# The second image's 3x3 convolution in tiles of 4 by 4 outputs instead of 4 by 2

## The chip, the cores and the metric

The kernel runs on one core of a Trainium2 chip. The time of a run is the device time of that core in microseconds; the time of a kernel is the median of its runs. A profile is one further execution, recorded by the hardware profiler.

Names of engines in what follows: PE is TensorE's matmuls and PEld its weight loads, DVE is VectorE, ACT is ScalarE, POOL is GpSimd, and SP is SyncE, which here only issues transfers.

## What is computed

Four images of 256 channels and 64 by 64 pixels, in fp32, go through four layers. Each layer normalises its input by groups of eight channels (`_gn`) and adds its result to it. Cut to what matters:

```python
# layer 0: a 3x3 convolution, group norm, relu, then attention over all 4096 pixels
xs = conv_general_dilated(x, smooth_w, (1, 1), padding='SAME') + smooth_b
xs = relu(group_norm(xs, gn1_w, gn1_b))
theta_x, phi_x, g_x = conv1x1(xs, ...)            # 128 channels each
attn = softmax(einsum('bnc,bcm->bnm', theta_x, phi_x))
y = einsum('bnm,bmc->bnc', attn, g_x)
x = x + group_norm(conv1x1(y, w_w, w_b)) * 0.1 + xs
# layer 1: linear attention; layer 2: generated depthwise and pointwise
# convolution; layer 3: a mixture of four 1x1 convolutions
```

The 3x3 convolution of layer 0 is what the change is about.

## The kernel before, in words

**Rounds.** The 256 channels are two halves of 128 partitions. Image 0's convolution runs first and alone (`convolve_first`), the prologue. Then come four rounds. Round b holds the attention of image b (`attend`): 8 blocks of 512 queries, each in 16 steps. A step makes two logits products `pf`, their exponentials `pr` on ACT (into `k4` buffers of 1024 elements), two products `py` with `g`, and adds `pr` to a running total `tot` on DVE. After a block, a product with ones sums `tot` over the partitions (`pss`), DVE takes the reciprocal and scales `py` into `yt`, and two products `ps_wy` follow; their statistics are taken on DVE and the result goes to `wy_d` in HBM.

**What runs beside the attention.** The order of every engine's work is written out by hand (`manual_schedule`): the engines take their instructions in program order. A `Chain` is a generator that yields prices; each unit of price times the chain's rate is one attention step. `later(n, f)` emits `f` after n further steps. In round 0 the chain is `scale_weights` and the convolution of image 1 at rate 1.5; in rounds 1 and 2 it is the rest of the layers of image b-1 (`tail`) and the convolution of image b+1 at rate 0.86; in round 3 the tail of image 2. The tail of image 3 runs alone at the end. Between the rounds `project` makes theta, phi and g from the convolved image in `big`.

**The convolution** (`convolve`) is of the Winograd kind: 4 output rows by 2 output columns at a time, that is 6 by 4 positions (`TY, MY, TX, MX = 6, 4, 4, 2`). For each of six row positions a, `down` combines input rows into `ra` (with `rt` between) on DVE. For each of four column positions k, `across` makes the moving operand `v` (two halves of 512) with one DVE operation:

```python
first, second, op = ((0, 2, ALU.subtract), (1, 2, ALU.add), (2, 1, ALU.subtract), (1, 3, ALU.subtract))[k]
tt(v.rearrange("p (h y x) -> p h y x", h=NH, x=IX), col(first), col(second), op)
```

`products` multiplies v by the transformed filters u: 2 output halves by 2 input halves, 4 matmuls of 512 columns into two banks, line 403:

```python
for oh in range(NH):
    for h in range(NH):
        nc.tensor.matmul(ps[oh], u(oh, h), v[:, bass.ts(h, 512)], start=(h == 0), stop=(h == NH - 1))
```

`joined` adds the four products into even and odd columns, and `joining` combines the six row positions into the four output rows in `big` (`image`). The emission of a product comes one step after its v, and its join one step later (`w.later(1, ...)`). DVE operations go through the helpers `tt` (line 118) and `stt` (line 121), so these two lines stand for many operations; the tile names tell them apart. `stats` (line 393) takes the statistics for the group norm, and `normed_relu` (line 492, ACT) finishes the image, each part of which is added to `xs_d` in HBM by a POOL transfer.

**Filters.** The transformed filters are made in the prologue from the 3x3 filters: `filter_down` makes the six rows `u1` (in `tpg`), and `filter_across` makes of each row the four column positions (lines 277 and after: one ACT and three DVE operations of 512 elements) and stores them in `filters` in HBM with eight transfers of 128 KB from SP. The prologue convolves image 0 in two forms: rows 3 and 4 with `products`, rows 0, 1, 2 and 5 with `row_products` (line 435; three horizontal taps in place, u1 as weights, copied from PSUM by ACT at line 440). Its v for row 3 is read from `rc`, a part of `big`. In rounds 0 to 2 `load_filters` brings the two u tiles of a product from `filters`, one product ahead.

Of the kernel before, what the change touches and what calls it, by code (L numbers as in the profile page):

```python
# [13 lines left out]
P = 128  # L14
# [20 lines left out]
TY, MY, TX, MX = 6, 4, 4, 2  # L35
IY, IX = HW // MY, HW // MX

# [53 lines left out]
def conv_preact_fast(ctx: ExitStack, tc: tile.TileContext, guard, x, wc, wtpg, ww, wqkv, wout, w1cat, wd2,  # L91
# [11 lines left out]
    def k4(name):  # L103
        return wk.tile([P, CH], F32, tag="k4", name=name, bufs=10)
# [3 lines left out]
    def k2(name):  # L108
        return wk.tile([P, 512], F32, tag="k2", name=name, bufs=6)
# [18 lines left out]
    big = cp.tile([P, NH, N], F32, name="big")  # L128
    tpg = cp.tile([P, 3, N], F32, name="tpg")
    ra = cp.tile([P, NH, IY, HW + 2], F32, name="ra")  # L130
    rt = cp.tile([P, NH, IY, HW], F32, name="rt")
# [24 lines left out]
    bigf = big.rearrange("p h n -> p (h n)")  # L156
# [79 lines left out]
    filters = tc.dram_tile([TY, NH, P, TX, NH, P], F32, name="filters")  # L236
# [30 lines left out]
    def filter_across(a, stay=False):  # L267

        ends = u1[:, a].rearrange("p h (j o) -> p h j o", j=3)
        s, mid = (t.rearrange("p (h o) -> p h o", h=NH)  # L270
                  for t in (wk.tile([P, 512], F32, tag="inv", name="ends2"), k2("middle") if a == 4 else junk()))
        if stay:
            both = [k2("both_u").rearrange("p (h o) -> p h o", h=NH) for _ in range(2)]
        else:
            t = k4("both_u").rearrange("p (b h o) -> p b h o", b=2, h=NH)
            both = [t[:, b] for b in range(2)]
        nc.scalar.mul(mid, ends[:, :, 1], 0.5)
        tt(s, ends[:, :, 0], ends[:, :, 2], ALU.add)
        stt(both[0], s, 0.5, mid, ALU.mult, ALU.add)
        stt(both[1], s, 0.5, mid, ALU.mult, ALU.subtract)  # L280

        def of(k):
            return both[k - 1] if k in (1, 2) else ends[:, :, 0 if k == 0 else 2]

        for oh in range(NH):
            for k in range(TX):
                nc.sync.dma_start(out=filters[a, oh, :, k], in_=of(k)[:, :, bass.ts(oh, P)])
        return lambda k, oh, h: of(k)[:, h, bass.ts(oh, P)]

# [60 lines left out]
    def rows_of(k, h=None):  # L350

        sel = slice(k, k + MY * (IY - 1) + 1, MY)
        return xp[:, :, sel, :] if h is None else xp[:, h, sel, :]
# [4 lines left out]
    def down(a, to, prior=None):  # L358

        A, T = inside(to), rt  # L360
        mul, add, sub = ALU.mult, ALU.add, ALU.subtract
        if a in (0, 5):
            lo = 0 if a == 0 else 1
            return [(stt, o, i, f, j, mul, add) for h in range(NH) for o, i, f, j in (
                (A[:, h], rows_of(lo + 2, h), -5.0, rows_of(lo + 4, h)), (A[:, h], rows_of(lo, h), 4.0, A[:, h]))]
# [6 lines left out]
        return [(stt, A[:, h], T[:, h], -2.0 if a == 2 else -4.0, inside(prior)[:, h], mul, add) for h in range(NH)]  # L372

    def across(k, rows):

        def col(j):
            return rows[:, :, :, j:j + MX * (IX - 1) + 1:MX]

        v = k4("v")
        first, second, op = ((0, 2, ALU.subtract), (1, 2, ALU.add), (2, 1, ALU.subtract), (1, 3, ALU.subtract))[k]  # L380
        tt(v.rearrange("p (h y x) -> p h y x", h=NH, x=IX), col(first), col(second), op)
        return v

    ACROSS = (1, 2, 0, 3)

    def joiner(st):
# [8 lines left out]
        def take(a, oh):  # L395
            dst[oh] = image[:, oh, :, a, :] if a in (0, 1, 3) else k4("t").rearrange("p (y x) -> p y x", x=HW)

        def products(a, k, v, u):

            ps = [bank("ps_conv") for _ in range(NH)]  # L400
            for oh in range(NH):
                for h in range(NH):
                    nc.tensor.matmul(ps[oh], u(oh, h), v[:, bass.ts(h, 512)], start=(h == 0), stop=(h == NH - 1))  # L403
                if k == 1:
                    one[oh] = k2("one").rearrange("p (y x) -> p y x", x=IX)
                    nc.scalar.copy(one[oh], ps[oh].rearrange("p (y x) -> p y x", x=IX))
            return ps

        def joined(a, k, ps):

            for oh in range(NH):
                p = ps[oh].rearrange("p (y x) -> p y x", x=IX)
# [3 lines left out]
                if k == 2:  # L416
# [26 lines left out]
        def joining(a, oh, t):  # L443

            y0, y1, y2, y3 = (image[:, oh, :, j, :] for j in range(MY))
            if a == 2:
                return [(tt, y2, y1, t, ALU.add), (tt, y1, y1, t, ALU.subtract), (tt, y0, y0, y2, ALU.add)]
            if a == 4:
                both = k4("both").rearrange("p (y x) -> p y x", x=HW)
                return [(tt, both, y3, t, ALU.add), (tt, y3, y3, t, ALU.subtract), (tt, y0, y0, both, ALU.add),  # L450
                        (stt, y2, both, 4.0, y2, ALU.mult, ALU.add), (stt, y1, y3, 2.0, y1, ALU.mult, ALU.add),
                        (stt, y3, y3, 6.0, y1, ALU.mult, ALU.add)]
            return [(tt, y3, y3, t, ALU.add)] if a == 5 else []

        def rows_joined(a, oh, t):
            for op, *args in joining(a, oh, t):
                op(*args)

        return products, joined, row_products, rows_joined, joining, stats

    def input_stats():
# [6 lines left out]
        return (yield from group_finish(st, avg8, 1e-5))  # L468

# [14 lines left out]
    def normed_relu(w, b, st):  # L484
# [3 lines left out]
        sc, sh = affine(gm, rstd, vec_s[:, V_G1W, :], vec_s[:, V_G1B, :], bias, 1.0)  # L488
        for c in range(N // CH):
# [6 lines left out]
    def convolve(w, b):  # L496

        _, gm, rstd = yield from input_stats()
        yield from normalise(gm, rstd)
        st = stats_tile()  # L500
        products, joined, _, rows_joined, joining, stats = joiner(st)
        PRODUCTS = [(a, k) for a in range(TY) for k in ACROSS]

# [32 lines left out]
        def load_filters(i):  # L536
            res = []
            for oh in range(NH):
                u = wk.tile([P, NH, P], F32, tag="u", name="u", bufs=4)
                nc.sync.dma_start(out=u, in_=filters[PRODUCTS[i][0], oh, :, PRODUCTS[i][1]])  # L540
                res.append(u)
            return lambda oh, h: res[oh][:, h, :]
# [3 lines left out]
        for i, (a, k) in enumerate(PRODUCTS):  # L546
            if k == 1:
                for op, *args in down(a, ra, ra):
                    op(*args)
                    yield 0.35  # L550
            v, u = across(k, ra), us
# [7 lines left out]

    def convolve_first(w):  # L560
# [5 lines left out]
        def across_all(a, rows):  # L566
            return [(a, k, across(k, rows), lambda oh, h, k=k: u[a](k, oh, h)) for k in ACROSS]

# [4 lines left out]
        products, joined, row_products, rows_joined, _, stats = joiner(st)  # L573
        go(down(0, ra))
        filter_down((1, 2))
        go(down(1, rb))
        filter_down((5,))
        filter_down((3, 4))
        u = {a: filter_across(a, stay=True) for a in (4, 3)}
# [6 lines left out]
        go(down(2, ra, rb))  # L586
        row_products(1, rb)
        go(down(3, rc))
        three = [(a, k, products(a, k, v, u)) for a, k, v, u in across_all(3, rc)]
        go(down(4, rb, rc))  # L590
        four = across_all(4, rb)
        go(down(5, rb))
        for i, (a, k, v, f) in enumerate(four):
            if i + 1 < TX:
                joined(*three[i + 1])
            filter_across((0, 1, 2, 5)[i])
# [3 lines left out]
        for i in range(1, TX):  # L600
# [460 lines left out]
    def mixed(w, b, big, k4, st, sh, held):  # L1061
# [39 lines left out]
        for h in range(NH):  # L1101
            wm.append(mix[:, h, :] if held is None else wk.tile([P, NH * P], F32, tag="u", name="wmh", bufs=4))
# [69 lines left out]
    with tc.manual_schedule(engines={E.PE, E.Activation, E.DVE, E.Pool, E.SP}):  # L1172
        run(Chain(convolve_first).steps())
        run(project())
        for b in range(B - 1):
            attention = attend(b)
            parts = [tail(b - 1, big, qT)] if b > 0 else [scale_weights]
            if b == 0:
                load_x(1)
            run(Chain(both(*parts, lambda w: convolve(w, b + 1)), 1.5 if b == 0 else 0.86).steps(), attention)  # L1180
# [605 lines left out]
```

## Time and profile before

| what | value |
|---|---|
| median of 3 runs | 3144.82 us (3144.27 to 3144.91) |
| the profiled execution | 3145.76 us, of which its span 3144.0 us |
| granted TensorE clock | 0.987 of full, mean over the span |
| prologue, up to the first `ps_tp` of image 0 | 146.1 us |
| round 0, first `pf` to the first `ps_tp` of image 1 | 190.9 to 738.5 us |
| `tot` on DVE, 1024 elements | x448, mean 1219 ns |
| `v` on DVE, 1024 elements | x72, mean 1219 ns |
| reciprocal on DVE, 512 elements | x32, mean 3352 ns |
| joins from PSUM on DVE, 512 elements | 682 to 684 ns |
| normalise on DVE, 1024 elements | x16, mean 807 ns |

How to read the page: a group row names line, engine, operation, output <- input by the program's names, shape and count, then busy time and the mean of one, then the engine's idle time before it and what ended that. Durations include a latency that overlaps the next instruction, so the distance from one start to the next is shorter than the mean of one. The chain of waits is followed back from the last instruction, each time to what released it. fp32 matmuls count two instructions each.

### The profile page before, as it was taken

The page shows a single profiled execution, that of the slowest core. Times are in us where ns is not written, and L with a number is a line of the kernel's source. Part 1 is how long each engine was busy: PE and PEld are TensorE (multiplying, and loading weights), DVE is VectorE, ACT ScalarE, POOL GpSimd, SP SyncE. Part 2 cuts the span into 40 slices and gives each one's busy share as a digit, 9 for nine tenths or more (in the row PEclk, how much of TensorE's full clock was granted, in tenths as well). Part 3 has the DMA queues.
Part 4 walks back from the last instruction along what each step waited for, and adds up shares of the span by engine and source line. Part 5 has one row for each costly group of instructions (what it writes and reads, how often), then busy time and mean ns, then how long its engine had stood idle before and what let it go on. Part 6 is the DMA issues. An engine that isn't in the chain of part 4 may idle for free.

```text
span 3144.0 us, 24213 instructions
## 1 busy us (share of the span) xinstructions
PE 3033.0 (96%) x8526; PEld 1472.9 (47%) x8526; DVE 2079.6 (66%) x2611; ACT 1129.2 (36%) x2097; POOL 131.6 (4%) x175
## 2 busy tenths in 40 slices
PE   6899999999999999999999999999999999996888
PEld 3454444445564444444565444444545544443533
DVE  8736766443547995877536896778363768855485
ACT  2233224332555332323364432222445443333510
POOL 0000000000010000000011000000100100000100
PEclk9999999999999999999999999999999999998999
DMA  5610013001100023113300102310410010120011
GB/s 184 182 34 26 32 35 66 7 14 47 67 11 21 20 74 116 39 39 67 114 8 3 41 20 77 110 44 31 113 62 1 11 34 14 47 74 34 14 60 65
DMA packets 73985, 161.68 MB, mean 51 GB/s; under 512 B 7936, under 2 KB 39424, under 8 KB 70912
## 3 DMA queue, kind: packets, MB, share of 16 engines
q1 hardware_dynamic: 69248, 143.27, 13.3%
q0 software_dynamic: 4608, 16.78, 2.9%
q8 instruction: 70, 1.15, 0.2%
q14 instruction: 59, 0.48, 0.0%
HBM read 103.40 MB, written 73.40 MB: 56 GB/s over the span
## 4 chain that ended last, share of the span: by engine, by line
PE 80%; DVE 12%; issue 5%; ACT 2%; DMA 0%; POOL 0%; SPq 0%; POOLq 0%; ACTq 0%
PE pf L655 23%; PE py L694 23%; PE ps_conv L403 8%; PE ps_qkv L784 5%; DVE dw L121 4%; PE ps_tp L631 4%; PE ps_ex L1117 3%; PE ps_pw L979 3%; DVE tot L118 2%; PE ps_g L636 2%; PE ps_wy L678 2%; PE ps_o L852 1%; PE ps_ctx L806 1%; PE ps_dw L1014 1%; PE ps_ss L770 1%
## 5 line engine op out<-in xcount | busy, mean ns | idle before, releaser
L656 ACT ACTIVATE pr<-pf 128x512 f32<-128x512 f32 x1024 | 604.2, 596 | 1227.3 <-PE pf L655 1214.2
L655 PE MATMUL pf<-tpg 128*128 128x512 f32 x2048 | 967.2, 595 | 1.4 <-ACT pr L656 1.4
L694 PE MATMUL py<-pr,tpg 128*128 128x512 f32 x2048 | 962.1, 592 | 3.0 <-ACT pr L656 2.9
L118 DVE TENSOR_TENSOR tot<-tot,pr 128x1024 f32<-128x1024 f32 x448 | 546.3, 1219 | 249.7 <-ACT pr L656 248.1
L694 PEld LDWEIGHTS py<-pr,tpg 128*128 128x128 f32 x2048 | 388.8, 190 | 494.3 <-issue 479.8
L655 PEld LDWEIGHTS pf<-tpg 128*128 128x128 f32 x2048 | 381.5, 190 | 443.0 <-issue 419.1
L121 DVE SCALAR_TENSOR_TENSOR dw<-xp,dk,dw 128x1008 f32<-128x1008 f32 x216 | 272.9, 1267 | 6.8 <-ACT dw L971 3.7
L403 PE MATMUL ps_conv<-v,u 128*128 128x512 f32 x576 | 259.0, 596 | 3.6 <-DVE v L118 3.6
L403 PEld LDWEIGHTS ps_conv<-v,u 128*128 128x128 f32 x576 | 109.7, 191 | 143.5 <-issue 136.6
L784 PE MATMUL ps_qkv<-wqkv_s,xg 128*128 128x384 f32 x384 | 129.9, 487 | 0.0
L631 PE MATMUL ps_tp<-big,wtpg_s 128*128 128x512 f32 x256 | 118.0, 605 | 3.0 <-ACT big L492 3.0
L118 DVE TENSOR_TENSOR tpg<-ps_g,bg_s 128x512 f32<-128x512 f32 x32 | 22.1, 691 | 145.6 <-PE ps_g L636 145.6
L210 POOL TENSOR_TENSOR rstd<-rstd,half 128x2 f32<-128x2 f32 x24 | 16.8, 700 | 2419.3 <-DVE rstd L315 2225.7
L979 PE MATMUL ps_pw<-dw,pk 128*128 128x512 f32 x224 | 104.6, 601 | 8.1 <-DVE dw L121 8.1
L669 DVE RECIPROCAL inv<-pss 128x512 f32<-128x512 f32 x32 | 107.3, 3352 | 7.2 <-PE pss L667 7.2
L784 PEld LDWEIGHTS ps_qkv<-wqkv_s,xg 128*128 128x128 f32 x384 | 72.2, 190 | 53.6 <-issue 9.6
L794 DVE TENSOR_REDUCE qs<-qk 128x16 f32<-128x512 f32 x24 | 16.5, 686 | 119.0 <-ACT qk L788 119.0
L118 DVE TENSOR_TENSOR v<-ra 128x1024 f32<-128x1024 f32 x72 | 86.7, 1219 | 0.4
L632 ACT ACTIVATE tpg<-ps_tp,btp_s 128x512 f32<-128x512 f32 x64 | 43.9, 687 | 119.6 <-PE ps_tp L631 119.6
L631 PEld LDWEIGHTS ps_tp<-big,wtpg_s 128*128 128x128 f32 x256 | 47.9, 195 | 55.0 <-issue 50.6
L854 ACT ACTIVATE junk<-ps_o 128x256 f32<-128x256 f32 x128 | 49.2, 384 | 67.5 <-PE ps_o L852 59.4
L979 PEld LDWEIGHTS ps_pw<-dw,pk 128*128 128x128 f32 x224 | 43.0, 192 | 62.6 <-issue 51.9
(281 smaller groups left out, 2904.6 us busy)
## 6 DMA issues: line engine op xcount, KB each, us to landing
u<-filters SPq DMA_DIRECT2D x144, 128.0 KB, 2.3
xp<-in_x_dram SPq DMA_DIRECT2D x16, 1024.0 KB, 6.3
xs_d<-big POOLq DMA_DIRECT2D x32, 512.0 KB, 11.7
wy_d<-wt SPq DMA_DIRECT2D x32, 512.0 KB, 3.0
out_dram<-res SPq DMA_DIRECT2D x64, 256.0 KB, 2.0
wy<-wy_d SPq DMA_DIRECT2D x28, 512.0 KB, 5.2
xs<-xs_d SPq DMA_DIRECT2D x24, 512.0 KB, 5.3
wp<-in_wp_dram SPq DMA_DIRECT2D x16, 512.0 KB, 4.6
```

What stands on the lines that cost most here:

```text
L118: nc.vector.tensor_tensor(o, a, b, op)
L121: nc.vector.scalar_tensor_tensor(o, a, s, b, op0, op1)
L403: nc.tensor.matmul(ps[oh], u(oh, h), v[:, bass.ts(h, 512)], start=(h == 0), stop=(h == NH - 1))
L631: nc.tensor.matmul(ps, wtpg_s[:, h, k, :], big[:, h, cols], start=(h == 0), stop=(h == NH - 1))
L636: nc.tensor.matmul(ps[:, j, :], big[:, h, bass.ts(4 * c + j, P)], wtpg_s[:, h, 2, :], start=(h == 0), stop=(h == NH - 1))
L655: nc.tensor.matmul(pf, phi[:, bass.ts(2 * m + s, P)], theta[:, bass.ts(q, 512)], start=True, stop=True)
L656: nc.scalar.activation(pr[:, bass.ts(s, 512)], pf, AF.Exp)
L669: nc.vector.reciprocal(inv, pss)
L694: nc.tensor.matmul(py, g[:, bass.ts(2 * m + s, P)], probs[i][:, bass.ts(s, 512)], start=(m == 0 and s == 0), stop=(m == NM - 1 and s == 1))
L784: nc.tensor.matmul(ps[:, 0:3 * HID], xg[:, h, bass.ts(j, P)], wqkv_s[:, h, :], start=(h == 0), stop=(h == NH - 1))
L979: nc.tensor.matmul(ps, pk[:, h * NH * P + oh * P:h * NH * P + (oh + 1) * P], dw[h][:, bass.ts(s, 512)], start=(h == 0), stop=(h == NH - 1))
L1117: nc.tensor.matmul(ps, wm[h][:, bass.ts(oh, P)], big[:, h, cols], start=(h == 0), stop=(h == NH - 1))
```

## The change

Only image 1's convolution (round 0) changes its form; images 2 and 3 keep 4 by 2 tiles. It takes 6 by 6 positions, in three pairs of column positions, (1,2), (3,4) and (0,5). The normalised input is written to `big` in a new place and order: every fourth pixel side by side (`planar`), so that a column position is 16 consecutive elements. The outputs go to where the input was (`xp`), and the last Relu puts them back in order into `big`. One set of filters serves both forms: `filter_across` for rows 0, 1, 2 and 5 and all stores of `filters` leave the prologue, which stores the six rows `u1` in `rows_d` instead (`keep`). `filters_across`, in round 0 ahead of the convolution, loads them back into `big`, makes four column positions of each on DVE, and stores these; the two outer ones are read from `rows_d`. The 4 by 2 form takes positions 0, 1, 2 and 3, of which 1 and 2 now carry a factor 0.5 at the join. Tiles u are of 512 elements and three, not of 256 and four; `k4` has 9 buffers for 10, `k2` has 5 for 6. `big` grows to (64+2) rows of 68. The chain of round 0 gets the rate 1.22.

```diff
-TY, MY, TX, MX = 6, 4, 4, 2
+TY, MY, TX, MX = 6, 4, 6, 4
 IY, IX = HW // MY, HW // MX
+TX1, MX1 = 4, 2
+RW = MX * (IX + 1)
...
-        return wk.tile([P, CH], F32, tag="k4", name=name, bufs=10)
+        return wk.tile([P, CH], F32, tag="k4", name=name, bufs=9)
...
-    big = cp.tile([P, NH, N], F32, name="big")
+    big_all = cp.tile([P, NH, (HW + 2) * RW], F32, name="big")
+    big = big_all[:, :, 0:N]
...
+    def filters_across(w):
+        n = NH * 3 * NH * P
+        def load(a):
+            t = big[:, a % 2, 0:n].rearrange("p (h j o) -> p h j o", h=NH, j=3)
+            nc.sync.dma_start(out=t, in_=rows_d[a])
+            return t
+        loaded = [load(0), load(1)]
+        yield 2
+        for a in range(TY):
+            t = loaded[a]
+            f = big[:, a % 2, n:n + (TX - 2) * NH * NH * P].rearrange("p (k h o) -> p k h o", k=TX - 2, h=NH)
+            first, mid, last = (t[:, :, j, :] for j in range(3))
+            for op, *args in ((tt, f[:, 0], first, last, ALU.add), (tt, f[:, 1], f[:, 0], mid, ALU.subtract),
+                              (tt, f[:, 0], f[:, 0], mid, ALU.add), (stt, f[:, 2], last, 4.0, first, ALU.mult, ALU.add),
+                              (stt, f[:, 3], mid, -2.0, f[:, 2], ALU.mult, ALU.add),
+                              (stt, f[:, 2], mid, 2.0, f[:, 2], ALU.mult, ALU.add)):
+                op(*args)
+                yield 0.3
+            if a + 2 < TY:
+                loaded.append(load(a + 2))
+            nc.sync.dma_start(out=filters[a], in_=f)
...
+        ops = {0: lambda: each(2, -5.0, col(4), col(5)) + each(0, 4.0, vt[:, 0], vt[:, 1]),
+               1: lambda: each(1, -4.0, col(3), col(4)) + [(tt, one, one, two, add), (stt, two, two, 2.0, one, mul, sub)],
+               3: lambda: [(tt, vt, cols(3), cols(1), sub), (stt, one, one, 2.0, two, mul, add),
+                           (stt, two, two, 2.0, one, mul, sub)]}
...
+        def products(pair, v, u):
+            banks = []
+            for i in range(2):
+                ps = bank("ps_conv")
+                for oh in range(NH):
+                    for h in range(NH):
+                        nc.tensor.matmul(ps[:, bass.ts(oh, IY * IX)], u[i][:, h, bass.ts(oh, P)],
+                                         v[:, i, bass.ts(h, IY * IX)], start=(h == 0), stop=(h == NH - 1))
+                banks.append(ps)
+            if pair != (0, 5):
+                parts[pair] = k4("sums").rearrange("p (k n) -> p k n", k=2)
+                nc.scalar.mul(parts[pair][:, 0], banks[0], -1 / 6 if pair == (1, 2) else 1 / 24)
+            return banks
...
+            if pair == (0, 5):
+                put((0, 0.25, ps[0], None), (3, 1.0, ps[1], None))
+            elif not end:
+                s = parts[pair]
+                f = -1 / 6 if pair == (1, 2) else 1 / 24
+                stt(s[:, 1], ps[1], -f, s[:, 0], ALU.mult, ALU.add)
+                stt(s[:, 0], ps[1], f, s[:, 0], ALU.mult, ALU.add)
+            else:
+                near, far = parts[1, 2], parts[3, 4]
+                put(*((j, f, far[:, j % 2], near[:, j % 2]) for j, f in enumerate((1.0, 2.0, 4.0, 8.0))))
...
+    def normalise_planar(gm, rstd):
...
+                src = xin[:, h, rows, :].rearrange("p y (i r) -> p y r i", r=MX)
+                to = planar[:, h, rows.start + 1:rows.stop + 1, :].rearrange("p y (r i) -> p y r i", r=MX)[:, :, :, 0:IX]
+                if h == 0:
+                    nc.vector.tensor_scalar(to, src, gm[:, 0:1], rstd[:, 0:1], ALU.subtract, ALU.mult)
+                else:
+                    nc.scalar.activation(to, src, AF.Identity, bias=nb[:, h:h + 1], scale=rstd[:, h:h + 1])
+            yield 1
...
+    def convolve_second(w):
...
+            elif a == 4:
+                for oh in range(NH):
+                    rest.extend(joining(a, oh, dst[oh]))
+                for j in range(4):
+                    w.later(1 + j, lambda: some(3))
+                for j in range(3):
+                    w.later(5 + j, lambda j=j: stats(j))
...
+            if pair == PAIRS[0]:
+                for op, *args in down(a, planar, ra, rt, ra):
+                    op(*args)
+                    yield 0.75
...
+            for op, *args in ops:
+                op(*args)
+                yield 0.4
+            w.later(1, lambda a=a, pair=pair, v=v, u=u: multiply(a, pair, v, u))
+            yield 1
...
-            parts = [tail(b - 1, big, qT)] if b > 0 else [scale_weights]
+            parts = [tail(b - 1, big, qT), lambda w: convolve(w, b + 1)] if b > 0 else [
+                scale_weights, filters_across, convolve_second]
...
-            run(Chain(both(*parts, lambda w: convolve(w, b + 1)), 1.5 if b == 0 else 0.86).steps(), attention)
+            run(Chain(both(*parts), 1.22 if b == 0 else 0.86).steps(), attention)
```

In the built program all engines' instructions keep the order in which this code emits them.

## The prediction

> **What bounds the kernel now.** I read the page first, then busy time by stretch of round 0 (the attention of image 0, with the convolution of image 1 beside it; 190.9 us is its first logits product, 738.5 us the end of its last), then the timelines of the waits found there.
>
> ```profile
> PE 3033.0 (96%) x8526; PEld 1472.9 (47%) x8526; DVE 2079.6 (66%) x2611; ACT 1129.2 (36%) x2097; POOL 131.6 (4%) x175
> PE 80%; DVE 12%; issue 5%; ACT 2%; DMA 0%; POOL 0%; SPq 0%; POOLq 0%; ACTq 0%
> L403 PE MATMUL ps_conv<-v,u 128*128 128x512 f32 x576 | 259.0, 596 | 3.6 <-DVE v L118 3.6
> ```
>
> ```profile
> 190.90:310.00 119.10, 119.10 (x284) 53.32 (x283) 78.96 (x95) 43.58 (x72) 0.71 (x1) 1.00 0.05 16
> 380.00:390.00 10.00, 8.10 (x20) 3.40 (x19) 10.00 (x10) 2.39 (x4) 0.00 (x0) 1.00 0.00 0
> 460.00:470.00 10.00, 8.35 (x21) 3.45 (x20) 9.93 (x9) 2.39 (x4) 0.00 (x0) 1.00 0.01 2
> 500.00:738.50 238.50, 238.50 (x560) 105.73 (x559) 105.56 (x105) 94.12 (x156) 7.65 (x9) 1.00 0.12 27
> ```
>
> The columns are the stretch, its length, then busy time of PE, PEld, DVE, ACT, POOL. PE is busy for all of round 0's 547.6 us but 3.55 us. Both holes lie where DVE is busy throughout, and both end with a v:
>
> ```profile
> 374.82 2.48 DVE L118 TENSOR_TENSOR big<-big,t 128x1024 f32<-128x1024 f32 x2
> 377.21 1.22 DVE L118 TENSOR_TENSOR ra<-xp 128x1024 f32<-128x1024 f32 x1
> 378.34 1.22 DVE L118 TENSOR_TENSOR rt<-xp 128x1024 f32<-128x1024 f32 x1
> 379.48 1.22 DVE L118 TENSOR_TENSOR tot<-tot,pr 128x1024 f32<-128x1024 f32 x1
> ...
> 388.56 1.22 DVE L118 TENSOR_TENSOR v<-ra 128x1024 f32<-128x1024 f32 x1
> ```
>
> ```profile
> 389.83 5.40 PE L403 MATMUL ps_conv<-v,u 128*128 128x512 f32 x8 [1.90 <-DVE v L118]
> ```
>
> So a matmul taken out of round 0 comes off the time, unless DVE, which serves the attention's totals and the convolution in one queue, falls behind.
>
> **PE work removed.** The old image 1 needs 24 products of 4 matmuls, 192 instructions of 512 columns (each fp32 matmul is two). The chain of waits has 8 of them in 3.43 us, 0.4292 us each: 82.4 us. The new one needs 6 by 6 positions by 4 matmuls by 2: 288 instructions of 256 columns. The nearest rows with another width scale with columns (the chain has 16 of ps_qkv, 384 columns, in 5.16 us; 16 of ps_g, 128 columns, in 1.78 us), so 0.2146 us each: 61.8 us. Gain **20.6 us**. [...] ps_g's 16 instructions, each with its own load of 128 columns, advance by 111 ns, and this does not hold the load's 192 ns as well. 256-column ones exist too, eight in 1.83 us to the next matmul, the first after a wait:
>
> ```profile
> 925.54 1.99 PE L852 MATMUL ps_o<-w,xp 128*128 128x256 f32 x8 [0.52 <-DVE w L121]
> 927.37 1.88 PE L655 MATMUL pf<-tpg 128*128 128x512 f32 x4
> ```
>
> I take 20.6.
>
> **Old waits of round 0**: both holes belong to the old order of DVE's work, and go: -3.6 us. What is late next follows.
>
> **New DVE work of round 0.** Down stays 24 operations, on 1088 elements for 1024. Across is 66 operations for 24. The joins, counted in the built order, are 24 on sums, 42 on the outputs in xp and 14 on rt, most of 512 elements. Filters_across adds 36 of 512 elements. From the starts above, an independent operation on 1024 advances DVE by 1.14 us (1.25 if it needs the one before), one on 512 by 0.61, so one on 1088 by 1.21. Together DVE rises from some 310 to 361 us, against some 527 us of PE: it has room on the average, and filters_across (three operations a step of 3.43 us, 1.8 us beside 1.14 of totals) and normalise_planar (one operation a step) are hidden. The latter reads every fourth fp32; no row has that. [...] The old v reads every second fp32 and costs the 1219 ns of a plain one[...]. The old row of this step is 0.81 us; even at 2.4 us it fits the 2.2 us that a step leaves, nearly, so I take nothing. The last Relus stand five steps (17 us) ahead of image 1's projection, in the built ScalarE order, so their strides are covered as well.
>
> Room on the average is not enough at one place. In the built order the twelve joins of row 4 and the statistics come right after the seventh query block's reciprocal. From there to the first half of row 5's first v, DVE has: reciprocal 3.39, yt 0.61, twelve joins of 1024 (six dependent) 14.3, two downs 2.4, three totals 3.4, two statistics of wt 1.2, three v operations 1.9: 27.2 us, starting 0.2 us after the reciprocal's product. PE has six steps of 3.43 and ps_wy's 1.72: 22.3 us. PE waits **5.1 us**. Then DVE has the rest of that v 0.7, three totals 3.4, twelve statistics 7.3, the next pair's difference and two operations 2.4, a pair of sums 1.5: 15.3 us, against PE's 3.43 + 6.87 + 1.72 = 12.0: **3.2 us** more. The same addition on the old order gives 2.0 and 1.7 us where the trace has 1.9 and 1.65, so I trust it to about 2 us. Elsewhere DVE's arrears stay under two steps. Sum +8.3 us; queued behind on DVE are the totals and the next reciprocal, and nobody else waits long.
>
> **The filters' way through HBM.** Keep stores the six rows (4.7 MB) in the prologue, in place of 48 stores of 128 KB on SP. Filters_across loads and stores some 11 MB through SP in about 45 us, 245 GB/s. Each DVE operation there waits in order for its load, with the totals behind it. In 100 to 120 us the trace moves 395 GB/s, and between 200 and 240 us now nothing, so I take 0; at the 187 GB/s of 80 to 100 us, the row with the most small transfers, each of six rows would be about 2.3 us late, less what slack holds: up to 5 us on PE. A pair needs two u tiles and there are three, so the second load of the next pair waits on SP for the current pair's first product, and a wy_d store may stand behind it. The next pair comes some three steps (10 us) later, and u's 128 KB land in 2.3 us, so this costs nothing.
>
> **Prologue.** Filter_across for rows 0, 1, 2, 5 leaves: 12 DVE operations of 0.61 and four of ScalarE, and their DMAs. PE runs without a hole from 47.8 to 137.3 us there, so this gains nothing. But the built program has one wait more. The first v of row 3 now waits for ScalarE's eighth copy of row products, which the old one did not (big's planes lie 4488 elements apart instead of 4096; the code gives no need for it).
>
> ```profile
> 63.49 0.59 ACT L440 COPY big<-ps_row 128x512 f32<-128x512 f32 x1 [4.56 <-PE ps_row L435]
> 68.64 0.59 ACT L440 COPY big<-ps_row 128x512 f32<-128x512 f32 x1 [4.56 <-PE ps_row L435]
> 70.36 0.59 ACT L406 COPY one<-ps_conv 128x512 f32<-128x512 f32 x1 [1.13 <-PE ps_conv L403]
> ```
>
> The old v is done by 60.3 us, the new one starts at 69.3 and ends at 70.5; PE was to go on at 68.4. **+2.1 us.** The other v behind it (1.14 each against PE's 3.43) catch up.
>
> **Rounds 1 and 2.** The factor 0.5 turns 24 joins each into scalar forms (683 ns to at most the 748 of the nearest PSUM row), two small memsets enter POOL, and k4 falls from 10 buffers to 9, so some exponentials may wait for a total two or three steps back. PE's idle there is about 7 us a round. I take +0.3 us, bounds 0 and 3.
>
> **Sum**: -20.6 - 3.6 + 8.3 + 2.1 + 0.3 = -13.5 us. The profiled execution has a span of 3144.0 us and 3145.76 us in all; 3144.0 - 13.5 = 3130.5, and 1.8 around it gives 3132.3. The median of the runs is 0.9 us below the profiled one: **3131 us**.
>
> **The rivals.**
> - VectorE keeps up (0.13): its operations overlap better than I add, the 8.3 us vanish: 3131 - 8.3 = 3123 us. For it: DVE is free 34% of the time. Against: the same addition finds the old waits.
> - VectorE or the filters' DMA are later than I add (0.16): up to 5 us by the DMA bound, or 10% dearer short-run operations (42 us of DVE in the critical stretch, so 4 us): about 3136 us.
> - Weight loads show at 256 columns[...] (0.06): [...] Against it are ps_g and ps_o.
> - Slower (0.04): the new operations run over rows of 16 elements, and no row has runs shorter than 32 outputs. The convolution's own DVE operations are some 133 us of 254 in a stretch of 355. At 1.7 times their price the stretch's 92 us of DVE room is used up and DVE becomes the bound; from 1.9 times on (254 + 0.9 x 133 = 374, 19 us over the stretch) the change is slower by more than 0.2%, and at 2.0 times (387, 32 us over) the time is 3163 us. Against: runs of 64 in rows of 66 cost 1219 ns, like flat ones.
> - The case of the sum (0.61): 3126 to 3135 us.
>
> 6.3 us (0.2%) is about what a measurement of this kernel can tell from no change. Below 3138.5 us lie the sum's case, the first rival and most of the second: faster 0.87; same 0.09; slower 0.04. The range, 3123 to 3139 us, reaches from the first rival to the end of the second.
>
> **What would show it.** Right: ps_conv of 256 columns near 0.215 us apart; round 0 about 531 us long; two PE waits on v near the seventh block, together 6 to 10 us, with DVE full; about 2 us of PE idle before the first ps_conv; rounds 1 to 3 as before. Wrong: PE waiting on yt or v early in round 0 (DMA), weight loads between conv matmuls, or v operations on 512 well above 0.69 us.

## The result and the profile after

The changed kernel takes **3126.92 us** (median of four runs, 3125.03 to 3129.2) against 3144.86 us for the kernel before (four runs of the same session, 3144.27 to 3146.62): 0.9942 of the time, 95% interval 0.9925 to 0.996. The forecast was 3131 us. The profiled execution took 3125.03 us, its span 3123.2 us.

The same two lines of the page as in the prediction, and the new form's row:

```profile
PE 3008.6 (96%) x8622; PEld 1492.7 (48%) x8622; DVE 2122.4 (68%) x2689; ACT 1138.1 (36%) x2101; POOL 130.9 (4%) x178
PE 76%; DVE 16%; issue 6%; ACT 2%; DMA 0%; POOL 0%; SPq 0%; POOLq 0%; ACTq 0%; DVEq 0%
L563 PE MATMUL ps_conv<-v,u 128*128 128x256 f32 x288 | 68.0, 391 | 5.3 <-DVE v L124 5.0
```

PE has 96 instructions more and 24 us less of busy time, and DVE has 43 us more. The 288 new instructions waited once for a v that was late, for 5.0 us.

To see where the time went, I cut the span at four places that all kernels here have: the first logits product `pf`, the first `ps_tp` of image 1 (end of round 0), the last `ps_wy` of image 3, and the end.

| stretch | before | after | difference |
|---|---|---|---|
| prologue, up to the first `pf` | 190.76 | 192.88 | +2.1 |
| round 0 | 547.62 | 529.71 | -17.9 |
| rounds 1 to 3, up to the last `ps_wy` | 2106.45 | 2106.96 | +0.5 |
| last stretch (image 3's last layers, alone) | 299.2 | 293.6 | -5.5 |
| span | 3144.0 | 3123.2 | -20.8 |

The last row but one is a surprise: the change does not touch that code. Up to there the change is worth 15.3 us; the forecast had 13.5.

**Round 0.** First the whole of it, before and after, by engine (columns as in the prediction: stretch, length, busy time of PE, PEld, DVE, ACT, POOL, then granted clock, DMA share, GB/s):

```profile
190.76:738.38 547.62, 544.07 (x1272) 241.00 (x1271) 323.98 (x344) 185.35 (x310) 8.36 (x10) 1.00 0.10 26
```

```profile
192.88:722.59 529.71, 524.45 (x1369) 261.14 (x1368) 373.31 (x434) 197.88 (x318) 7.14 (x9) 0.99 0.20 59
```

DVE's work grew by 49 us (forecast: 51) and is still far below PE's. PE has few holes. Its timeline in the changed kernel, where they are:

```profile
615.07 1.88 PE L933 MATMUL py<-pr,tpg 128*128 128x512 f32 x4
621.98 6.26 PE L563 MATMUL ps_conv<-v,u 128*128 128x256 f32 x16 [5.03 <-DVE v L124]
628.08 1.88 PE L894 MATMUL pf<-tpg 128*128 128x512 f32 x4
...
634.94 1.89 PE L563 MATMUL ps_conv<-v,u 128*128 128x256 f32 x8
637.06 1.97 PE L563 MATMUL ps_conv<-v,u 128*128 128x256 f32 x8 [0.23 <-PE ps_conv L563]
```

DVE's timeline just ahead of the wait's end:

```profile
618.85 2.48 DVE L127 SCALAR_TENSOR_TENSOR xp<-xp 128x1024 f32<-128x1024 f32 x2
621.24 0.69 DVE L124 TENSOR_TENSOR v<-v 128x512 f32<-128x512 f32 x1
```

The last of row 4's twelve joins (`xp<-xp`) stand in DVE's queue right ahead of the v that PE needs, as the prediction said, and the wait is 5.03 us where it had 5.1. The second wait that it had, 3.2 us at row 5's second pair, is only 0.23 us at 637.06. But there is something else: the sixteen products after the wait take 6.10 us from start to next start. Elsewhere in this round sixteen take 3.45 (a line of the chain of waits, then the stretches around the pause). The granted clock, the third column from the end, tells why:

```profile
335.12 3.45 PE ps_conv L563 x16
```

```profile
616.90:620.30 3.40, 0.05 (x1) 0.00 (x0) 3.37 (x4) 0.00 (x0) 0.00 (x0) 1.00 0.00 0
620.30:627.15 6.85, 5.17 (x12) 4.19 (x13) 6.82 (x9) 0.60 (x1) 0.00 (x0) 0.50 0.03 9
```

3.4 us into the pause the clock falls to half, and it stays there for 6.8 us, 5.2 of them with work in hand: 2.65 us lost. The kernel before shows the same on a small scale. After its pause of 1.90 us the eight products at 389.83, shown in the prediction, took 5.24 us to the next start, not 3.43. First the stretch with the pause, then the one at half clock:

```profile
387.30:390.71 3.41, 1.51 (x4) 0.49 (x3) 3.41 (x4) 0.00 (x0) 0.00 (x0) 1.00 0.00 0
390.71:394.12 3.41, 3.41 (x5) 1.33 (x4) 3.41 (x4) 0.59 (x1) 0.00 (x0) 0.50 0.04 13
```

So round 0 adds up: products 82.4 - 62.1 = -20.3; old waits -3.55, and -1.8 for the clock behind the first; new wait +5.03, clock behind it +2.65, and +0.23. Together -17.7, measured -17.9.

**Prologue.** The predicted wait is there. ScalarE's eighth copy, the v behind it, and PE's product that waits for that v:

```profile
69.37 0.58 ACT L535 COPY big<-ps_row 128x512 f32<-128x512 f32 x1 [4.57 <-PE ps_row L530]
```

```profile
69.99 4.64 DVE L124 TENSOR_TENSOR v<-big 128x1024 f32<-128x1024 f32 x4 [10.67 <-ACT big L535]
```

```profile
71.27 7.13 PE L491 MATMUL ps_conv<-v,both_u 128*128 128x512 f32 x16 [1.94 <-DVE v L124]
```

### The profile page after: what moved, and what is told of

Same layout as the page of the kernel before. It is cut to its first block, busy times and chain, and to the rows that moved or that the text cites. A ratio compares the mean times of both kernels' runs of the same rounds, so it can differ in the third digit from the quotient of the medians.

```text
span 3123.2 us, 24290 instructions
## 1 busy us (share of the span) xinstructions
PE 3008.6 (96%) x8622; PEld 1492.7 (48%) x8622; DVE 2122.4 (68%) x2689; ACT 1138.1 (36%) x2101; POOL 130.9 (4%) x178
## 4 chain that ended last, share of the span: by engine, by line
PE 76%; DVE 16%; issue 6%; ACT 2%; DMA 0%; POOL 0%; SPq 0%; POOLq 0%; ACTq 0%; DVEq 0%
PE pf L894 22%; PE py L933 22%; PE ps_qkv L1023 5%; PE ps_conv L491 4%; DVE dw L127 4%; PE ps_tp L870 4%; PE ps_ex L1356 3%; DVE tot L124 3%; PE ps_pw L1218 3%; PE ps_conv L563 2%; PE ps_g L875 2%; PE ps_o L1091 1%; PE ps_wy L917 1%; DVE big L127 1%; PE ps_ctx L1045 1%
## 5 line engine op out<-in xcount | busy, mean ns | idle before, releaser
L491 PE MATMUL ps_conv<-v,u 128*128 128x512 f32 x384 | 170.8, 593 | 0.0
L491 PEld LDWEIGHTS ps_conv<-v,u 128*128 128x128 f32 x384 | 72.9, 190 | 92.0 <-issue 91.1
L563 PE MATMUL ps_conv<-v,u 128*128 128x256 f32 x288 | 68.0, 391 | 5.3 <-DVE v L124 5.0
```

The costliest lines, as they stand in the source:

```text
L563: nc.tensor.matmul(ps[:, bass.ts(oh, IY * IX)], u[i][:, h, bass.ts(oh, P)], v[:, i, bass.ts(h, IY * IX)], start=(h == 0), stop=(h == NH - 1))
```

## The experiments

My theory after this reading: the stage sums hold; what I had left out is the clock, which charged a second time for two pauses (2.65 us behind the one of 5.03 us, 1.8 us behind the one of 1.90 us); and the last stretch's 5.5 us are the clock too, not the change. The rivals are written with each run. All kernels below were profiled, and their stretches are set together here, since totals alone cannot tell effects of 2 us:

| kernel | median of runs | first `pf` | round 0 | rounds 1 to 3 | last stretch |
|---|---|---|---|---|---|
| before, first profile | 3144.86 (4) | 190.76 | 547.62 | 2106.45 | 299.2 |
| before_again | 3144.96 (1) | 191.20 | 545.94 | 2106.45 | 299.6 |
| changed, first profile | 3126.92 (4) | 192.88 | 529.71 | 2106.96 | 293.6 |
| after_again | 3128.74 (5) | 195.12 | 529.71 | 2107.06 | 298.9 |
| no_copy_wait | 3129.88 (5) | 191.28 | 529.72 | 2106.95 | 299.8 |
| fill_new_hole | 3132.74 (5) | 192.24 | 531.39 | 2106.98 | 300.4 |
| spread_joins | 3124.14 (5) | 191.99 | 521.41 | 2106.96 | 299.9 |
| before_filled | 3144.33 (13) | 191.42 | 545.94 | 2106.48 | 296.5 |
| tail_spin | 3128.85 (5) | 193.09 | 529.70 | 2107.03 | 297.5 |
| filters_alone | 3144.72 (13) | 193.07 | 546.04 | 2107.14 | 298.5 |
| split_products | 3133.51 (6) | 192.11 | 531.69 | 2106.98 | 299.6 |
| best | 3119.76 (5) | 191.48 | 521.41 | 2106.92 | 298.2 |
| best_spin | 3119.59 (5) | 190.88 | 521.41 | 2106.92 | 298.6 |

**The changed kernel with PE kept busy in the new hole.** In `products`, ahead of a bank's own matmuls; `extra` is 5 for row 5's first pair and 0 elsewhere.

```diff
+                for _ in range(extra if i == 0 else 0):
+                    nc.tensor.matmul(ps, ones, phi[:, 0:512], start=True, stop=True)
```

> The changed kernel with five more matmuls of 512 columns (4.29 us by the 0.429 us per two instructions of the chain) put on PE ahead of the first product of row 5, the one that waits 5.03 us for v; their result is overwritten. In the profile the 16 products after that wait take 6.1 us where 16 elsewhere take 3.45. Theory: they are slow because the granted clock falls to 0.5 after a pause, so with PE kept busy they take 3.45 us and round 0 ends 2.65 us sooner although work was added: 526.9 us for 529.6, 3124.3 us. Rival: the second half of the pair waits for DVE and the clock has no part: the row takes 6.1 us still, round 0 stays 529.6 us or grows, 3127 us or more.

Measured: round 0 took 531.39 us, 1.7 more, and the runs 3132.74 us (ratio to before 0.9963, 0.995 to 0.9977). PE's timeline:

```profile
616.15 4.46 PE L562 MATMUL ps_conv<-tpg,ones 128*128 128x512 f32 x10
621.34 3.72 PE L565 MATMUL ps_conv<-v,u 128*128 128x256 f32 x16 [0.73 <-DVE v L124]
624.90 1.88 PE L896 MATMUL pf<-tpg 128*128 128x512 f32 x4
...
631.76 1.89 PE L565 MATMUL ps_conv<-v,u 128*128 128x256 f32 x8
636.42 3.52 PE L565 MATMUL ps_conv<-v,u 128*128 128x256 f32 x8 [2.77 <-issue]
639.73 2.06 PE L896 MATMUL pf<-tpg 128*128 128x512 f32 x4
```

Both theories of the expectation are half right. The row was slow because of the clock: with PE busy ahead of them, the sixteen products take 3.56 us instead of 6.10, and the granted clock is 1.00 from 621.3 to 633.6 us. But the total did not fall, because PE now came to the second pair 2.5 us sooner and had to wait there for 2.77 us: this is the second wait of the prediction, 3.2 us. The trace does not name what ended that wait, but DVE's last operation on that v (`v<-v`) runs from 635.64 to 636.32 us, and PE starts at 636.42. Half clock follows this pause of 2.77 us again: the granted clock is 0.55 from 636.9 to 640.4 us, and 8 products take 3.31 us for 1.72. In the changed kernel the clock's loss after the first wait had hidden the second.

**Row 4's joins and statistics spread out.**

```diff
-                for j in range(4):
-                    w.later(1 + j, lambda: some(3))
+                for j in range(6):
+                    w.later(1 + 2 * j, lambda: some(2))
                 for j in range(3):
-                    w.later(5 + j, lambda j=j: stats(j))
+                    w.later(13 + j, lambda j=j: stats(j))
```

> The changed kernel with the twelve joins of row 4 emitted two at a time in every second step (three at a time in four steps before) and the twelve statistics after them, from the thirteenth step on; no work is added or taken away. Theory: the 5.03 us wait, the 2.65 us of half clock behind it and the 0.23 us after that come only from these joins standing ahead of row 5's first v, so all 7.9 us go: round 0 521.7 us for 529.6, 3119.0 us. Rival: VectorE is the bound of that whole stretch and the wait only moves to a later product of row 5 or to the end of round 0: at least 4 us of it come back, 3123 us or more.

Measured: round 0 521.41 us, 8.3 less, no wait in it, and row 5's first products at full pace, sixteen in 3.46 us:

```profile
615.90 3.62 PE L563 MATMUL ps_conv<-v,u 128*128 128x256 f32 x16
619.36 1.88 PE L894 MATMUL pf<-tpg 128*128 128x512 f32 x4
```

So the wait, and the clock's loss behind it, came only from the order of DVE's work, and VectorE was not the bound. The rival is excluded for round 0. The runs, though, took 3124.14 us (ratio 0.9934, 0.9921 to 0.9948), some 4 us less than the changed kernel's (3127.7 over its nine runs), not 8: the profile's last stretch is 6.3 us longer than in the changed kernel's first profile.

**The kernel before with PE kept busy in its first hole, and the kernel before once more.** The edit is that of fill_new_hole, with two matmuls ahead of the product of (a, k) = (3, 1).

> The kernel before with two more matmuls of 512 columns (1.72 us) on PE ahead of the product that waits 1.90 us for v at 389.8 us; their result is overwritten. After that wait eight products took 5.24 us where eight take 3.43. Theory: the pause of 1.9 us cost 1.8 us more in granted clock, so the prediction's value of this old wait (1.9) was half of what removing it is worth (3.7): round 0 545.7 us for 547.5, 3143.0 us. Rival: the clock's fall there is not caused by so short a pause: eight products still take 5.2 us, round 0 547.5, 3144.8 us or a little more.

> The kernel before, as it is, for one more profile. Theory: its waits of 1.90 and 1.65 us in round 0 stand where they stood, since the order of the work makes them, but the half clock behind the first (1.8 us) [...] may be missing or stand behind the other: round 0 545.7 to 549.5 us. The last stretch takes 294 to 301 us. Rival: each part of the first profile comes back to within 0.3 us: 547.6 and 299.2 us.

Measured: before_filled has 545.94 us in round 0, 1.7 less than the first profile, as the theory wants. But the unedited kernel, profiled again, has 545.94 us as well, with both pauses in place:

```profile
390.28 3.70 PE L403 MATMUL ps_conv<-v,u 128*128 128x512 f32 x8 [1.90 <-DVE v L118]
393.81 1.88 PE L655 MATMUL pf<-tpg 128*128 128x512 f32 x4
```

The same pause of 1.90 us, and this time eight products in 3.53 us, at a granted clock of 1.00 from 390.28 to 393.81 us; in the first profile it was 0.50 from 390.71 to 394.12 us. So half clock followed this pause in one execution and not in the other. What decides between the two is not shown. What filling it saves is 1.8 us in one execution and nothing in another; the medians (3144.33 and 3144.5, ratio 0.9999, 0.999 to 1.0007) show no difference.

**The changed kernel without the wait for ScalarE's copy.** The wait hangs on the layout of `big`. Here the two planes share a zero row, so that `big` has 35 x 256 elements and not 2 x 4488 = 8976. Which property of the layout brings the wait is not shown.

```diff
-    big_all = cp.tile([P, NH, (HW + 2) * RW], F32, name="big")
-    big = big_all[:, :, 0:N]
+    bigf = cp.tile([P, 35 * 256], F32, name="big")
+    big = bigf[:, 0:NH * N].rearrange("p (h n) -> p h n", h=NH)
...
-    planar = big_all.rearrange("p h (y x) -> p h y x", x=RW)
+    lines = bigf[:, 0:(NH * (HW + 1) + 1) * RW].rearrange("p (y x) -> p y x", x=RW)
```

Plane h of `planar` is then rows h x 65 to h x 65 + 65 of `lines`.

> The changed kernel with the planes of big laid out so that the first v of row 3 does not wait for ScalarE's eighth copy of row products (nothing else changed). My theory: that wait cost PE 2.1 us and nothing later covers it. So the first logits product moves from 193.0 to 190.9 us, round 0 stays 529.6 us long, and the time falls by 2.1 us, from 3126.9 to 3124.8 us. Rival: the wait is made good further on in the prologue (the joins and the Relus of image 0 on DVE and ACT come last there anyway): first logits product at 193, 3126.9 us.

```profile
68.85 7.03 PE L496 MATMUL ps_conv<-v,both_u 128*128 128x512 f32 x16
```

The wait is gone. From the start of the row products ahead of it (`ps_row` from `tpg`) to this `ps_conv` PE takes 20.6 us, as in all profiles without the wait, and 22.7 in all seven with it: 2.1 us, as the theory had it. The first `pf` shows this less sharply. It comes at 191.28 us here and at 190.76 to 191.48 in the other five without the wait, but at 191.99 to 193.09 in six with it. In the seventh, after_again, it comes at 195.12, because half clock follows the wait (the granted clock is 0.51 from 72.8 to 76.3 us, and sixteen products take 8.67 us to the next start, not 6.97). Later in the prologue PE pauses for 3.95 us with the wait and without it. The changed kernel's first profile has a granted clock of 0.50 from within that pause on, from 142.5 to 152.7 us. The first eight `ps_tp` products take 5.16 us to the next start there, 4.93 in after_again and 6.15 in no_copy_wait; the next eight take 3.43 in all three. The rival, that the wait is made good further on, finds no support: no wait of PE grows shorter there. The total, 3129.88 us (ratio 0.9952, 0.9939 to 0.9966), does not show the 2 us; its last stretch took 299.8 us.

**The filters' way alone.** Round 0 convolves image 1 in the old tiles, with everything that concerns filters as in the change. (The first pair of lines brings back the old last Relus.)

```diff
-        if b == 1:
+        if b < 0:
...
-                scale_weights, filters_across, convolve_second]
+                scale_weights, filters_across, lambda w: convolve(w, 1)]
...
-            run(Chain(both(*parts), 1.22 if b == 0 else 0.86).steps(), attention)
+            run(Chain(both(*parts), 1.5 if b == 0 else 0.86).steps(), attention)
```

> One part of the change alone: filters_across, keep and the one set of filters, but image 1 convolved in tiles of 4 by 2 as before (round 0 at a rate of 1.5). Theory: the filters' way costs 2.1 us in the prologue and nothing in round 0 by itself; the old waits of 3.6 us and the clock's loss move with the order of DVE's work, one wait of some 2.4 us being left: first logits product at 193, round 0 between 545 and 549 us, 3143 to 3147 us. Rival: its transfers hold up DVE, which waits for them in order (up to 5 us on PE): round 0 550 us or more, 3149 us.

Measured as the theory had it: first `pf` 193.07 us, round 0 546.04 us, 3144.72 us (ratio 1.0004, 0.9996 to 1.0013). PE's only wait in round 0 is one for a v:

```profile
535.16 5.39 PE L491 MATMUL ps_conv<-v,u 128*128 128x512 f32 x8 [2.43 <-DVE v L124]
```

So loading, combining and storing the filters added no wait on PE: this one, with the half clock behind it (0.51 from 535.2 to 538.7 us; the eight products take 5.23 us to the next start), stands in place of the two old ones. In the changed kernel DVE waited once in that work, by the trace for a store of filters (`filters<-big`), and PE did not notice:

```profile
L124 DVE TENSOR_TENSOR big<-big 128x512 f32<-128x512 f32 x18 | 12.4, 687 | 3.7 <-DMA filters<-big 3.5
```

**Twice as many weight loads.**

```diff
-                    for h in range(NH):
-                        nc.tensor.matmul(ps[:, bass.ts(oh, IY * IX)], u[i][:, h, bass.ts(oh, P)],
-                                         v[:, i, bass.ts(h, IY * IX)], start=(h == 0), stop=(h == NH - 1))
+                    for part in range(2):
+                        for h in range(NH):
+                            nc.tensor.matmul(ps[:, bass.ts(2 * oh + part, P)], u[i][:, h, bass.ts(oh, P)],
+                                             v[:, i, bass.ts(2 * h + part, P)], start=(h == 0), stop=(h == NH - 1))
```

> The changed kernel with each of its products of 256 columns cut in two of 128 columns, so the same columns with twice the weight loads (576 instructions for 288, each with its load). Theory: PE advances by columns, as ps_g's rows of 128 columns do (0.111 us each): 576 x 0.1113 = 64.1 us for 62.1, so 2 us more in round 0, 531.6 us, 3129 us. Rival: weight loads of full tiles do not overlap[...].

Measured: round 0 531.69 us, 2.0 more than the changed kernel. The group's row of that profile:

```profile
L564 PE MATMUL ps_conv<-v,u 128*128 128x128 f32 x576 | 69.1, 279 | 6.1 <-DVE v L124 5.0 <-issue 1.0
```

288 weight loads were added and cost 2.0 us in all. The chain of waits has the 32 matmuls of a pair in 3.57 us, for 3.45 before. That is 2.1 us in 18 pairs. A load takes 192 ns in this trace (the median of 576), and the matmuls, each with its own load, advance by 112 ns: the loads of these full tiles lie under the matmuls. The 288 added loads end to end would have been 55 us (an estimate, 288 times 192 ns). (The runs took 3133.51 us, ratio 0.9967, 0.9955 to 0.9979; again the last stretch, 299.6 us, is at its long end.)

**The last stretch: the changed kernel again, and with PE kept busy ahead of it.** For tail_spin two idle matmuls follow each part of image 3 that DVE finishes:

```diff
+        spin = bank("ps_spin") if xs_in is not None else None
...
             stt(big[:, h, cols], wy, sc[:, h:h + 1], xs, ALU.mult, ALU.add)
+            for s in range(2 if xs_in is not None else 0):
+                nc.tensor.matmul(spin, ones, big[:, h, bass.ts(2 * c + s, 512)], start=True, stop=True)
```

> The changed kernel as it is, once more. In the profiles so far the stretch from the last ps_wy product to the end, whose code all kernels here share, took 299.2 us (before), 293.6 (changed kernel), 299.9, 300.4, 299.9 and 296.5 us, with the granted clock. Theory: this stretch varies with where the clock's falls land, and the changed kernel's first profile was at the low end; its round 0 takes 529.6 us again, the last stretch 294 to 300 us, and the median lies between 3126 and 3130 us. Rival: the change has made the end itself shorter by 5.5 us: the last stretch takes 293.6 us again.

> The changed kernel with sixteen more matmuls of 512 columns on PE in its pause of 18.8 us ahead of image 3's linear attention (two for each part that VectorE finishes; their result is not used). Theory: the half clock after the pause is what makes the last stretch vary; with PE kept busy it runs its first products at full clock and the last stretch takes 293 to 295 us, about 3124 to 3126 us in all, with less scatter than the changed kernel alone. Rival: the scatter has another source (DMA or the later pauses), or PE's extra work delays the products: 3127 us or more, last stretch 296 us or more.

Measured: after_again 3128.74 us (3125.32 to 3134.63; ratio 0.995, 0.9936 to 0.9963). Its last stretch takes 298.9 us, with the same instructions in the same order. The start of the linear attention shows how; first the changed kernel's first profile, then after_again's:

```profile
2867.05 4.12 PE L1023 MATMUL ps_qkv<-wqkv_s,ra 128*128 128x384 f32 x12
2871.00 0.95 PE L1009 MATMUL ps_ss<-ones,s 128*128 128x1 f32 x8
```

```profile
2870.09 6.61 PE L1023 MATMUL ps_qkv<-wqkv_s,ra 128*128 128x384 f32 x12
2876.53 0.95 PE L1009 MATMUL ps_ss<-ones,s 128*128 128x1 f32 x8
```

The same pause of 18.84 us ends 7.7 and 8.4 us before these lines, and the other waits of the stretch are the same, to 0.1 us, in both. In the first the twelve products take 3.95 us to the next start, and the granted clock is 0.86 from 2863.5 to 2873.5 us; in the second they take 6.44, at 0.54 from 2866 to 2876 us. From the end of the pause to the `ps_ss` that follows them it is 11.69 us in the first and 14.87 in the second: 3.2 of the 5.3 us between these two stretches. Over the whole stretch PE worked for 25.9 us at half clock in the changed kernel's first profile and for 35.3 in the first profile of before. Half of the difference, 4.7 us, is most of the 5.5 us between them. So the 5.5 us of the first comparison are no effect of the change: its first profile has the shortest last stretch of all thirteen. The longest half clock of the stretch lies differently in the two. In the first profile of before it takes 27.3 us, from 2858.5 to 2885.9 us, and the twelve products start within it (at 2883.04 us, 5.34 us to the next start). In the changed kernel's first it takes 20.5 us, from 2845.8 to 2866.3 us, and ends before they start. With PE busy in the pause (tail_spin) the twelve products take 3.96 us to the next start again, from 2867.17 us on, but this did not make the kernel faster: 3128.85 us (ratio 0.9949, 0.9936 to 0.9963), last stretch 297.5 us. The rival holds: the time is lost further on in that stretch as well, where the granted clock is 0.80 from 2965 to 3000 us. The runs of tail_spin lie closer together (3127.41 to 3129.87), which five runs do not prove.

**Both repairs together.** The edits of spread_joins and no_copy_wait; best_spin adds that of tail_spin.

> The changed kernel with both repairs: row 4's joins and statistics spread out, and big laid out so that row 3's first v does not wait for ScalarE. Theory: the two gains measured by stage add, 8.2 us in round 0 and 1.6 to 2.1 us in the prologue: first logits product near 191.2 us, round 0 521.5 us; from the 3127.7 us that the nine runs of the changed kernel have as their median that makes 3118 us. Rival: the last stretch takes back a part, as it did with spread_joins alone (8.2 us of round 0 became some 4 us of the whole): 3121 to 3123 us.

> The kernel best with the sixteen idle matmuls of tail_spin in image 3's pause as well. Theory after tail_spin: they keep the clock up for the first products only, the falls further on stay; the time is that of best within 2 us. Rival: the long half-clock stretch of 27 us, which four of the profiles had and the changed kernel's first had not, is what the last stretch loses: last stretch 295 us or less and 4 us below best.

Measured: best 3119.76 us (3118.05 to 3123.18; ratio to before 0.9924, 0.9911 to 0.9938), best_spin 3119.59 us (0.992, 0.9907 to 0.9934). Round 0 of best, in the columns used above:

```profile
191.48:712.89 521.41, 521.41 (x1368) 258.99 (x1367) 372.56 (x434) 197.98 (x318) 7.15 (x10) 1.00 0.20 60
```

PE is busy in every microsecond of it, at full clock. Best is faster than both kernels, by some 8 us than the changed one (3127.7 us over its nine runs); the stages say 8.3 + 1.6 to 2.1. Idle matmuls in the last stretch gain nothing: in best_spin the mean granted clock is 0.88 from 2820 to 2860 us and 0.99 from 2860 to 2890 us, which leaves about 10 us of half clock there (my estimate from these means) and no stretch of 27 us, and the last stretch still takes 298.6 us, so the rival is out.

## Why the prediction was right, point by point

- **PE work, -20.6: right.** The chain of the changed kernel has 16 products in 3.45 us, 0.2156 each, 62.1 us in all, so -20.3. The 96 more weight loads at 256 columns did not show (62.1 us for a forecast of 61.8), and 288 more at 128 columns, in split_products, cost 2.0 us together.
- **Old waits, -3.6: right in place, too small in size.** They are 3.55 us, but behind one of them the clock cost another 1.8 us in the execution that I predicted from, and nothing in the next one. This is the term of the sum that was mis-sized, and the reason is one: I charged a pause with its length only. The clock's part stood in the very line that I showed, 5.40 us for eight products.
- **New waits, +8.3: right in sum, partly by luck.** 5.1 us came out at 5.03. The 3.2 us did not show as a wait, because half clock after the first wait, which the sum did not have, cost 2.65 us and let DVE catch up; fill_new_hole brought the second wait out at 2.77. Together it is 7.9 us. That the sum still came out is DVE's doing: its order of work sets when the second pair can begin, however PE spends the time before, and spread_joins gives back 8.3.
- **Filters, 0: right**, by filters_alone, and by the one DMA wait of 3.5 us on DVE that PE does not see.
- **Prologue, +2.1: right**, by no_copy_wait: 22.7 us with the wait and 20.6 without. In after_again the clock added 1.7 us.
- **Rounds 1 and 2, +0.3: right**, +0.5 with round 3.
- **DVE's short runs**: v operations on rows of 16 elements take 684 to 688 ns for 512, like flat ones, so the slower rival had no ground. (Its own sum has a slip: a stretch of 355 us with 254 us of DVE work leaves 101 us, not 92, so DVE would have become the bound at 1.76 times the price, not 1.7.) Normalise with every fourth element takes 1230 ns for 807, inside the 0.81 to 2.4 us that I had allowed, and PE does not wait for it.

The stages up to the last `ps_wy` give -15.3 us against the first profile of before, and -14.0 against the second (+1.7 - 16.2 + 0.5), for a forecast of -13.5. The medians differ by 17.9 us (interval 12.6 to 23.6), or by 17.2 with all nine runs of the changed kernel. What lies between is within what the last stretch does by itself from execution to execution, 293.6 to 300.4 us, so I count none of it for the change. The totals of spread_joins, no_copy_wait, fill_new_hole and split_products lie 3 to 5 us above what their stages and the changed kernel's nine runs say. The two first profiles tie the length of a last stretch to the time that PE works at half clock in it (35.3 us in the stretch of 299.2 us, 25.9 in that of 293.6). Whether it is longer in most runs of those kernels, and why, stays open.

## What to carry to other kernels

Charge a pause of PE with its length and with the clock that may fall behind it, here 1.6 to 2.65 us more behind pauses of 1.90 to 5.03 us; read this in the rows just after the wait (how long do sixteen products take there?). An engine that has room on the average can still make another wait where a block of its work is emitted together; spreading that block cost nothing and gave 8.3 us in round 0, where the whole change had given 17.9 (of the whole kernel's time, some 4 us). And before a difference of a few microseconds is believed, cut the spans at common places: a stretch that the change does not touch may differ by more than the effect.

## What the runs showed of the hardware

- The granted clock fell to half in or behind pauses of PE of 2.43 us (filters_alone, 0.51 over 3.5 us), 2.77 us (fill_new_hole, 0.55 over 3.5 us), 3.95 us (prologue of the first profiles of before and of the changed kernel, 0.50 for 10.2 us, with pauses of 0.93 and about 3.0 us in it) and 5.03 us (the changed kernel's first profile, 0.50 for 6.8 us). Behind a pause of 1.90 us it was 0.50 for 3.4 us in one profile of the kernel before and 1.00 in the other; behind one of 1.93 us it was 0.51 over 3.5 us in after_again, and behind one of 1.94 us 1.00 in the changed kernel's first profile. Behind one of 1.65 us in the first profile of before it was 1.00.
- Where half clock followed a pause in round 0, it cost 1.6 us (fill_new_hole), 1.8 us (before, filters_alone) and 2.65 us (the changed kernel).
- In split_products 288 more weight loads of full fp32 tiles cost 2.0 us together; a load takes 192 ns there, and the matmuls advance by 112 ns.
- A DVE tensor_scalar that reads every fourth fp32 and writes runs of 16 took 1230 ns for 1024 elements in the changed kernel; the one of the kernel before, which reads and writes them in a row, took 807. Operations that make `v` from runs of 16 elements took 684 to 688 ns for 512; flat ones (`big<-big`) took 687 and 688.
- A stretch of 300 us with many pauses varied by 6.8 us between executions with the same instructions in it (293.6 us in the changed kernel's first profile, 300.4 in fill_new_hole).
